# Attention outputs of six batches by seven products, with all slots of four engines in a written order

## The chip, the cores and the metric

The kernel runs on one NeuronCore of a Trainium2 chip, as a single program with one launch. The metric is device time in microseconds (us) of that core. Before the change three runs took 1434.19, 1436.90 and 1437.84 us, so the median is 1436.9 us. The profile is of one further execution, which took 1433.48 us with a span of 1431.7 us from its first to its last instruction.

A core has a matrix engine (PE, with PEld for its weight loads), a vector engine (DVE), a scalar engine (ACT), a general engine (POOL) and a queue that issues transfers (SP). Each works through its own instruction queue. Products are written to PSUM; in this program DVE and ACT take them out of it, and POOL works on SBUF alone.

## The reference, cut to what matters

Tokens are 8 batches of 512, each of 512 features, all float32. Two layers of cross attention stand in the network, each followed by a feed-forward part (a routed one after the first, a channel mix after the second). With a context of 120 keys for each batch and 16 heads of 32 features, a layer of attention is

```python
q = _split_heads(Q @ W_q.T)                  # Q is the layer norm of x
k = _split_heads(K @ W_k.T)                  # K and V are the context
v = _split_heads(V @ W_v.T)
scores = jnp.einsum('bhqd,bhkd->bhqk', q, k) / jnp.sqrt(jnp.float32(D_K))
probs = jax.nn.softmax(scores, axis=-1)
out = jnp.einsum('bhqk,bhkd->bhqd', probs, v)
out = out.transpose(0, 2, 1, 3).reshape(B, S, H * dk)
return out @ W_o.T                           # added to x, times tanh(gate)
```

The second layer adds biases and a mask over the keys. The change is about the last line, `out @ W_o.T`, and about the order in which everything in these two layers is issued.

## The kernel before, in words

**Tiling.** `x` stays in SBUF for the whole program as 32 tiles of 128 tokens, four to a batch. In a layer of attention (`CrossAttention`) keys and values are projected first (`project_keys`, `project_values`: one product of 120 x 512 for each batch), and then the tiles are worked through one by one.

**Queries.** For a whole batch they are computed by seven products of 256 x 256 blocks in place of eight (`SevenProducts`, Strassen's scheme in Winograd's form). `multiply` (line 149) issues four matmuls of 256 columns into one PSUM bank. The pieces `p1` to `p7` take the products out of PSUM and add them up. The sums of inputs that some products need (`left_steps`, `right_steps`) are made by DVE or POOL.

**Attention of a tile.** `scores` (line 489) fills two PSUM tiles of two banks each (pool `p_s`, two tiles in all, so one tile of tokens fills the pool). DVE takes the negative maxima (`nmx`, line 514) of the second of them, ACT runs eight exponentials over it (line 517), DVE takes the maxima (line 525) of the first and subtracts them (line 527), and ACT exponentiates the result (line 528). The step called `rest` takes reciprocals of the sums on DVE and multiplies on POOL (line 507, twice for a tile, 128 x 960 each). `transpose_probs` (line 546) turns the probabilities by 16 transposes into the same two PSUM tiles of `p_s`; `transpose_probs_late` (line 567) does so into four banks of the other pool, `p_mm`, which has four banks and serves everything else. `attend` (line 581) multiplies by the values, ACT copies the result to `aT` (line 589), and `output` (line 598) multiplies it with `wo`: four matmuls of 512 columns for each tile, after which DVE adds `gate` times the result to `x` (line 607).

**Slots.** `run` (line 617) is a loop of slots. Slot t holds the scores of tile t+1, a few products of queries of the next batch, the output of tile t-1 in two parts, the transposes and the attention of tile t, and the transposes of normalised `x` (`transpose_x`, line 421) of tile t+9. Between them `after(t, stage)` calls the next part of the network: in the first layer `RoutedFfn.in_slot` (statistics, the normalisation `route_norm` on ACT (line 714), transposes `route_x` (line 722) and logits `route_logits` (line 731), once for each tile); in the second `ChannelMix.in_slot`. `tail` works through the last slots.

**What sets the order.** `tc.manual_schedule(engines=...)` keeps the named engines in the order of the source. Around `run` it names PE alone in the first layer, and PE and SP in the second; a planner puts the instructions of DVE, ACT and POOL in order by its own estimate of when they can run. The construction before `run` and the tail behind it are in source order on the four compute engines.

Of the kernel before, what the change touches and what calls it, by code (L numbers as in the profile page):

```python
# [17 lines left out]
P = 128  # L18
# [53 lines left out]
class SevenProducts:  # L72
# [24 lines left out]
    @staticmethod  # L97
    def right_steps(w, t1, t2, t3, t4, engine):

        b11, b12, b21, b22 = [quarter(w, c, h) for c in (0, 1) for h in (0, 1)]

        def step(*args):
            return lambda: engine.tensor_tensor(*args)

        return [
            step(t3, b22, b12, ALU.subtract),  # L110
            step(t1, b12, b11, ALU.subtract),
            step(t2, b22, t1, ALU.subtract),
            step(t4, t2, b21, ALU.subtract),
        ]
# [91 lines left out]

class CrossAttention:
# [7 lines left out]
    def __init__(  # L215
# [20 lines left out]
        self.xn, self.xnT, self.qT, self.probs, self.aT = {}, {}, {}, {}, {}  # L236
        self.ops = {}
# [4 lines left out]
        with right("at_v") as self.vp:  # L242
            with right("at_k") as self.kp:
                self.load(ins, list(loads), mask, biases)
                if self.biased:
                    self.scale_biases()
                self.project_keys()
                if self.biased:
                    nc.gpsimd.tensor_scalar(self.gbo, self.gbo, self.gate, None, ALU.mult)
                for t in range(2):  # L250
                    self.normalize(t)
                if self.masked:
                    self.make_mask()
                self.sum_query_weights()
                for b in (1, 2):
                    self.stats_of_batch(b)
            self.work = pool("at_work", 2)
            self.prologue()

    def load(self, ins, loads, mask, biases):  # L260
# [4 lines left out]

        wv = self.soft.tile([P, NC * D], FP, name="wv", tag="pr")
        self.wv = wv.rearrange("p (c f) -> p c f", c=NC)
# [89 lines left out]
    def project_values(self, b):  # L357
# [15 lines left out]
        if b + 3 < B:  # L373
            self.stats_of_batch(b + 3)

    def prologue(self):

        for b in range(3):
            self.project_values(b)
        for t in range(2 * TB):  # L380
            self.transpose_x(t)
            self.normalize(t + 2)
            if t < TB - 1:
                self.project_values(t + 3)
            elif t < 2 * TB - 1:
                self.queries(0, t + 1 - TB)
        rest = self.scores(0)
        for b in range(B - 2, B):
            self.project_values(b)
        rest()  # L390

# [21 lines left out]
    def transpose_x(self, t):  # L413
        nc = self.nc
        b, i = divmod(t, TB)
        if i == 0:
            self.xnT[b] = self.work.tile([P, NC, S + 1], FP, name="xnT")
# [4 lines left out]
        nc.scalar.copy(self.xnT[b][:, :, i * P : (i + 1) * P], ps)  # L422
        if i == TB - 1:
            self.start_queries(b)
# [9 lines left out]

    def start_queries(self, b):

        xnT = self.xnT[b][:, :, :S]
        own = self.work.tile([P, 2, 256], FP, name="xns", bufs=1)
        sums = [quarter(xnT, 0, 1), quarter(xnT, 0, 0), own, quarter(xnT, 1, 0)]
        engine = self.nc.gpsimd if b > 1 else self.nc.vector  # L440
# [4 lines left out]
        self.xn7 = SevenProducts.right(xnT, *sums)  # L445

    def queries(self, b, f):

        if f == 0:
            self.qT[b] = self.work.tile([P, NC, S], FP, name="qT")  # L450
            self.q7 = SevenProducts(
                self.nc,
                lambda: self.p_mm.tile([P, 2, 256], FP, name="qps", tag="mm"),
                self.wq7,
                self.xn7,
                {(i, j): quarter(self.qT[b], i, j) for i in (0, 1) for j in (0, 1)},
                lambda: quarter(self.xnT[b], 0, 1),
                bias=(self.bqk[:, 0, 0:2], self.bmore) if self.biased else None,
            )
        self.q7.next(2 if f < TB - 1 else 1)  # L460
        if f == 0:
            for step in self.later_sums:
                step()

    def scores(self, t):
# [65 lines left out]
        def rest():  # L531
            norm(slice(2, 4))
            nc.vector.tensor_reduce(sm[:, :2, :], pv, AX.X, ALU.add)  # L533
            norm(slice(0, 2))
# [24 lines left out]
    def transpose_probs_late(self, t):  # L559
# [4 lines left out]
        for j in (2, 3, 0, 1):  # L564
# [3 lines left out]
            if j == 2:  # L568
# [5 lines left out]
    def attend(self, t):  # L574
# [13 lines left out]
        self.aT[t] = self.work.tile([P, NC, P], FP, name="aT")  # L588
        nc.scalar.copy(self.aT[t], aps)  # L589

    def output(self, t, chunks):

        nc, x = self.nc, self.cm.x
        if 0 in chunks:
            self.ops[t] = self.p_mm.tile([P, D], FP, name="ops", tag="mm")
        ops = self.ops[t]
        for c in chunks:
            nc.tensor.matmul(  # L598
                ops,
                self.aT[t][:, c, :],  # L600
                self.wo[:, c, :],
                start=(c == 0),
                stop=(c == NC - 1),
            )
        if NC - 1 in chunks:
            del self.ops[t], self.aT[t]
            nc.vector.scalar_tensor_tensor(
                x[:, t, :], ops, self.gate, x[:, t, :], ALU.mult, ALU.add
            )
# [7 lines left out]
    def run(self):  # L617

        for t in range(-1, NT - TB - 1):
            if t >= 0:  # L620
                if t + 10 < NT:
                    self.normalize(t + 10)
                self.scores(t + 1)()
            self.queries(*divmod(t + TB + 1, TB))
            self.after(t, 0)


            short = t % TB == TB - 2
            ahead = 3 if short else 2
            if t > 0:  # L630
                self.output(t - 1, range(ahead))
            x_ahead = short and not self.masked
            if x_ahead and t + 9 < NT:
                self.transpose_x(t + 9)
            if t >= 0:
                self.transpose_probs(t)
            if t > 0:
                self.output(t - 1, range(ahead, NC))
            if t + 9 < NT and not x_ahead:
                self.transpose_x(t + 9)  # L640
            self.after(t, 1)
            if t >= 0:
                self.attend(t)
            self.after(t, 2)

    def tail(self):

        for t in range(NT - TB - 1, NT + 1):
# [3 lines left out]
            self.output(t - 1, range(NC))  # L652
# [9 lines left out]
class RoutedFfn:  # L662
# [19 lines left out]

    def start(self):
# [22 lines left out]
    def route_stats(self, t):  # L706
        layernorm_sums(self.cm, self.route, t)
        layernorm_scales(self.cm, self.route, t, 1)

    def route_norm(self, t):  # L710

        nc, x = self.nc, self.cm.x[:, t, :]
        nc.sync.dma_start(out=self.aside[t * P : (t + 1) * P, :], in_=x)
# [41 lines left out]

    def in_slot(self, s, attention, stage):

        last = NT - TB - 1
        if stage == 2 and 0 <= s - 1:
            self.route_stats(s - 1)  # L760
        if (stage == 2 and (0 <= s - 1 < last - 1 or s == NT)) or (stage == 3 and s > last):
            self.route_norm(s - 1 if stage == 2 else s - 2)
        if stage != (0 if s == NT else 1):
            return
# [703 lines left out]
```

## Time and profile before

| what | us |
|---|---|
| median of three runs | 1436.9 |
| the profiled execution | 1433.48 |
| its span | 1431.7 |
| PE busy | 1384.2 (97%) |
| DVE busy | 1025.1 (72%) |
| ACT busy | 772.3 (54%) |
| POOL busy | 643.9 (45%) |
| one batch of the first layer's slots | 49.5 |
| one batch of the second layer's slots | 44.4 |

The first layer of attention lies from the start to about 475 us, the routed part up to 690 us, the second layer up to about 1138 us, and the channel mix behind that. The last two rows are the distance between the same instruction in two following batches (the products of queries that begin at 162.47, 212.01, 261.55 us in the first layer, and at 838.86, 883.22, 927.59 us in the second). A matmul's row in the profile is a little longer than its share of the time, since matmuls overlap; the distance between the starts of two rows is what a piece of work costs.

### The profile page before, as it was taken

To read this page: it belongs to the slowest core of one execution; us is meant where nothing else is said; L and a number is where in the kernel's file an instruction comes from. 1 tells how busy PE (TensorE), PEld (TensorE's weight loads), DVE (VectorE), ACT (ScalarE), POOL (GpSimd) and SP (SyncE) were. 2 spreads that over 40 slices of the span, in tenths; PEclk is the share of its full clock that TensorE was granted. 3 is DMA by queue.
4 is the path that set the end of the run, shared out by engine and by line. 5 is a ranking of instruction groups with operands and counts; after the bars stand their busy time and mean duration, and the time that the engine had idled before them with its cause. 6 is when DMAs were issued, how large, how long until landed. Compare 5 with 4: busy or idle time off the path is not lost.

```text
span 1431.7 us, 32559 instructions
## 1 busy us (share of the span) xinstructions
PE 1384.2 (97%) x13728; PEld 1068.2 (75%) x13728; DVE 1025.1 (72%) x1457; ACT 772.3 (54%) x1874; POOL 643.9 (45%) x576
## 2 busy tenths in 40 slices
PE   7999999999999998999999999999998999999997
PEld 3577777777776787888557777777776788888886
DVE  2666777777777676777576777777778588887786
ACT  1256666666666445444225665666656555445543
POOL 1425545545443001555375665665646333343331
PEclk9999999999999999999999999999999999999999
DMA  9200000000001347433301000000000000000001
GB/s 300 107 9 24 24 23 23 24 23 16 24 31 46 127 135 231 120 105 87 117 0 60 2 1 2 1 2 2 2 30 2 1 30 30 31 30 30 30 16 45
DMA packets 44886, 69.46 MB, mean 49 GB/s; under 512 B 2891, under 2 KB 20811, under 8 KB 44739
## 3 DMA queue, kind: packets, MB, share of 16 engines
q1 hardware_dynamic: 44451, 67.37, 14.6%
q8 instruction: 108, 1.77, 0.5%
q14 instruction: 39, 0.32, 0.1%
q10 hardware_dynamic: 288, 0.00, 0.0%
HBM read 50.59 MB, written 16.78 MB: 47 GB/s over the span
## 4 chain that ended last, share of the span: by engine, by line
PE 72%; DVE 14%; ACT 6%; POOL 4%; issue 3%; DMA 1%; POOLq 0%; DVEq 0%; ACTq 0%
PE ops L598 15%; PE qps L149 13%; PE tps L546 6%; PE cps L149 5%; PE aps L581 5%; PE s L489 4%; PE kps L342 4%; PE rps L992 3%; PE vps L361 3%; PE rlps L731 2%; PE l1ps L907 2%; PE ops L1013 2%; PE xnps L421 2%; PE l2ps L959 2%; PE gps L880 2%
## 5 line engine op out<-in xcount | busy, mean ns | idle before, releaser
L507 POOL TENSOR_TENSOR pr<-pr,rs 128x960 f32<-128x960 f32 x128 | 228.8, 1790 | 251.9 <-DVE rs L506 233.5
L598 PE MATMUL ops<-wo,aT 128*128 128x512 f32 x512 | 239.6, 594 | 0.7 <-ACT aT L589 0.7
L517 ACT ACTIVATE pr<-s,nmx 128x120 f32<-128x120 f32 x512 | 177.4, 372 | 114.0 <-DVE nmx L514 107.8
L598 PEld LDWEIGHTS ops<-wo,aT 128*128 128x128 f32 x512 | 92.1, 190 | 71.9 <-issue 67.0
L1005 POOL TENSOR_TENSOR r<-r,b 128x1024 f32<-128x1024 f32 x31 | 73.5, 2377 | 142.6 <-ACT r L1004 142.6
L149 PE MATMUL qps<-xnT,wq 128*128 128x256 f32 x512 | 119.6, 381 | 0.0
L546 PEld LDWEIGHTS tps<-ident,pr 128*120 128x120 f32 x864 | 96.8, 138 | 29.5 <-issue 26.2
L525 DVE TENSOR_REDUCE mx<-s 128x8 f32<-128x960 f32 x64 | 74.0, 1156 | 56.9 <-PE s L489 56.9
L517 ACT ACTIVATION_READ_ACCUMULATOR pr<-s,nmx 128x1 f32 x512 | 111.3, 217 | 0.0
L546 PE MATMUL tps<-ident,pr 128*120 128x128 f32 x864 | 104.7, 273 | 2.5 <-ACT pr L517 1.4
L149 PEld LDWEIGHTS qps<-xnT,wq 128*128 128x128 f32 x512 | 95.7, 189 | 15.2 <-issue 1.0
L533 DVE TENSOR_REDUCE sm<-pr 128x8 f32<-128x960 f32 x64 | 73.6, 1150 | 22.1 <-ACT pr L528 22.0
L49 DVE BATCH_NORM_STATS2 bnst<-x 128x6 f32<-128x512 f32 x128 | 86.8, 678 | 1.3
L422 ACT COPY xnT<-xnps 128x512 f32<-128x512 f32 x64 | 38.1, 595 | 82.0 <-PE xnps L421 82.0
L514 DVE TENSOR_REDUCE nmx<-s 128x8 f32<-128x960 f32 x64 | 73.5, 1149 | 6.8 <-PE s L489 6.8
L581 PE MATMUL aps<-prT,v 120*32 120x128 f32 x2048 | 73.3, 278 | 4.5 <-ACT prT L571 2.6
L527 DVE TENSOR_TENSOR pr<-s,mx 128x960 f32<-128x960 f32 x64 | 73.6, 1150 | 0.9
L1258 POOL TENSOR_TENSOR x<-x,cv 128x512 f32<-128x512 f32 x28 | 41.4, 1479 | 70.8 <-DVE cv L1255 70.8
L556 ACT COPY prT<-tps 120x1024 f32<-120x1024 f32 x54 | 55.0, 1019 | 32.9 <-PE tps L546 32.9
L489 PE MATMUL s<-kT,qT 32*128 32x120 f32 x2048 | 71.4, 276 | 0.0
L489 PEld LDWEIGHTS s<-kT,qT 32*128 32x128 f32 x2048 | 66.1, 187 | 6.5 <-issue 6.3
L581 PEld LDWEIGHTS aps<-prT,v 120*32 120x32 f32 x2048 | 53.8, 110 | 18.8 <-issue 8.3
(189 smaller groups left out, 3101.1 us busy)
## 6 DMA issues: line engine op xcount, KB each, us to landing
w<-in_w_dram SPq DMA_DIRECT2D x32, 512.0 KB, 4.8
x<-in_x_dram SPq DMA_DIRECT2D x8, 1024.0 KB, 15.4
aside<-x SPq DMA_DIRECT2D x32, 256.0 KB, 2.0
x<-aside SPq DMA_DIRECT2D x8, 1024.0 KB, 9.8
out_dram<-x SPq DMA_DIRECT2D x14, 512.0 KB, 2.8
ctx<-in_ctx_dram SPq DMA_DIRECT2D x4, 960.0 KB, 11.8
wk<-in_wk_dram SPq DMA_DIRECT2D x3, 1024.0 KB, 11.1
wv<-in_wv_dram SPq DMA_DIRECT2D x3, 1024.0 KB, 5.5
```

The source lines that it names most:

```text
L49: cm.nc.vector.bn_stats(st, cm.x[:, t, :])
L149: self.nc.tensor.matmul(ps[:, m, :], self.a[a][:, k, m * P : (m + 1) * P], self.b[b][:, k, :], start=(k == 0), stop=(k == 1),)
L489: nc.tensor.matmul(s[j // 2][:, j % 2, hc * LK : (hc + 1) * LK], self.qT[b][r : r + 32, hc, toks], self.kT[r : r + 32, hc, keys], start=no ...
L507: nc.gpsimd.tensor_tensor(pr[:, js, :, :], pr[:, js, :, :], rs[:, js, :, :].to_broadcast([P, 2, NC, LK]), ALU.mult,)
L514: nc.vector.tensor_reduce(nmx, sv[1], AX.X, ALU.max, negate=True)
L517: nc.scalar.activation(pr[:, 2 + j, hc, :], sv[1][:, j, hc, :], AF.Exp, bias=nmx[:, j, hc, :], accum_out=sm[:, 2 + j, hc : hc + 1],)
L525: nc.vector.tensor_reduce(mx, sv[0], AX.X, ALU.max)
L527: nc.vector.tensor_tensor(pv, sv[0], mx.to_broadcast([P, 2, NC, LK]), ALU.subtract)
L533: nc.vector.tensor_reduce(sm[:, :2, :], pv, AX.X, ALU.add)
L546: nc.tensor.transpose(ps[:, jj, hc * P : (hc + 1) * P], pr[:, 2 * u + jj, hc, :], self.cm.ident,)
L581: nc.tensor.matmul(aps[32 * j : 32 * j + 32, hc, :], self.v[b // 2][:LK, b % 2, h * HD : (h + 1) * HD], prT[:, j, hc, :], start=True, stop ...
L598: nc.tensor.matmul(ops, self.aT[t][:, c, :], self.wo[:, c, :], start=(c == 0), stop=(c == NC - 1),)
```

## The change

It has four parts.

1. **Outputs by seven products.** The outputs of batches 0 to 5 in each layer are no longer computed tile by tile. `aT` now holds the four tiles of a batch, and a new class, `SevenAdded`, multiplies it with `wo` by seven products, each scaled by the gate and added to `x`. Batches 6 and 7 keep `output`. The sums of `wo` are made once for each layer by POOL, in the buffer that held `wv`; the sums of `aT` are made by POOL in each of the six batches.
2. **A written order.** `run` is a list of slots of two kinds, `slot` and `short_slot`, and the four compute engines all follow the source.
3. **First slots.** The projections of the values of batches 4 to 7 move from ahead of the first slot into slots 0, 1 and 2; all seven products of the queries of batch 0 come one after another ahead of the scores; and `xnT` (normalised `x`, transposed) has one buffer in place of two.
4. **The next part of the network.** In the first layer `route_norm` of a tile moves to stage 0 of the slot in which `route_x` transposes it; the pieces of the routed part come two slots later than before and catch up at the end. In the second, statistics and transposes are spread differently over the last slots.

```diff
+class SevenAdded(SevenProducts):
+    def add(self, c, ps):
+        self.nc.vector.scalar_tensor_tensor(c, ps, self.gate, c, ALU.mult, ALU.add)
+    def add_sum(self, *places):
+        for c in places:
+            self.nc.gpsimd.tensor_tensor(c, c, self.t, ALU.add)
+    def p1(self):
+        ps = self.multiply("A11", "B11")
+        self.nc.scalar.activation(self.t, ps, AF.Copy, scale=self.gate)
+        self.add_sum(self.c[0, 0])
+    def p2(self):
+        self.add(self.c[0, 0], self.multiply("A12", "B21"))
+    def p5(self):
+        ps = self.multiply("S1", "T1")
+        self.add(self.c[0, 1], ps)
+        self.add(self.c[1, 1], ps)
+    def p6(self):
+        self.add(self.t, self.multiply("S2", "T2"))
+        self.add_sum(self.c[0, 1])
+    def p7(self):
+        self.add(self.t, self.multiply("S3", "T3"))
+        self.add_sum(self.c[1, 0], self.c[1, 1])
+    def p3(self):
+        self.add(self.c[0, 1], self.multiply("S4", "B22"))
+    def p4(self):
+        self.add(self.c[1, 0], self.multiply("A22", "T4"))
...
     def run(self):
+        self.slot(0, [(self.queries, 2), (self.project_values, 4)], [(self.queries, 1)])
+        self.normalize(2 * TB)
+        values = [(self.project_values, b) for b in (5, 6)]
+        self.slot(1, [(self.queries, 1)] + values, [(self.queries, 1)])
+        self.normalize(2 * TB + 1)
+        self.short_slot(
+            2, [(self.queries, 1)], [(self.project_values, B - 1), (self.end_of_values,)]
+        )
+        for b in range(B - 2):
+            t = TB * b + TB - 1
+            tile = TB * (b + 2)
+            last = b == B - 3
+            self.start_outputs(b)
+            outputs, queries = self.o7.next, self.queries
+            self.short_slot(
+                t,
+                [(self.transpose_x, tile), (self.normalize, tile + 2),
+                 (self.transpose_x, tile + 1)],
+                [(outputs,), (self.normalize, tile + 3), (self.transpose_x, tile + 2)],
+                [(queries, 1)],
+            )
+            self.slot(
+                t + 1,
+                [(outputs,), (self.transpose_x, tile + 3), (outputs, 2)],
+                [(outputs,)],
+            )
...
+            self.slot(
+                t + 2,
+                [(outputs,), (self.start_queries, b + 2), (outputs,), (queries, 1)],
+                [(queries, 1)] + [(self.output, t + 1)] * last,
+            )
...
+            self.slot(
+                t + 3,
+                [(queries, 3)],
+                [(queries, 1)] + [(queries, 1), (self.output, t + 2)] * last,
+            )
+
+    def end_of_values(self):
+        self.values.close()
+        self.sum_output_weights()
+        self.after(-1, 1)
+
+    def slot(self, t, ahead, behind):
+        rest = self.scores(t + 1)
+        self.issue(ahead)
+        self.after(t, 0)
+        rest(0)
+        self.transpose_probs(t)
+        rest(1)
+        self.issue(behind)
+        self.after(t, 1)
+        self.attend(t)
+        self.after(t, 2)
+
+    def short_slot(self, t, ahead, behind, first=()):
+        self.issue(first)
+        self.transpose_probs_late(t, (2, 3, 0))
+        self.issue(ahead)
+        self.attend(t)
+        if t % TB == TB - 1:
+            for step in self.output_sums:
+                step()
+        rest = self.scores(t + 1)
+        self.issue(behind)
+        self.after(t, 0)
+        self.after(t, 1)
+        rest(0)
+        rest(1)
+        self.after(t, 2)
...
-            with tc.manual_schedule(engines={engines.PE}):
+            with tc.manual_schedule(engines=compute):
                 attention.run()
-            with tc.manual_schedule(engines=compute):
                 attention.tail()
...
-        with tc.manual_schedule(engines={engines.PE, engines.SP}):
+        with tc.manual_schedule(engines=compute):
             attention.run()
-        with tc.manual_schedule(engines=compute):
             attention.tail()
             mix.run()
```

The prologue, `sum_output_weights` and `in_slot` of the routed part, in the new form:

```diff
     def prologue(self):
+        for b in range(2):
             self.project_values(b)
+        for t in range(TB):
             self.transpose_x(t)
             self.normalize(t + 2)
+            if t == 1:
+                self.project_values(2)
+        self.start_queries(0)
+        self.queries(6)
+        self.project_values(3)
+        self.queries(1)
+        for t in range(TB, 2 * TB):
+            self.transpose_x(t)
+            if t + 2 < 2 * TB:
+                self.normalize(t + 2)
+            if t == TB + 1:
+                rest = self.scores(0)
+        self.start_queries(1)
         rest()
+        self.stats_of_batch(B - 1)
...
+    def sum_output_weights(self):
+        w = self.wo
+        sums = self.xp.tile([P, 4, 2, 256], FP, name="wos", tag="xa")
+        sums = [sums[:, i] for i in range(4)]
+        for step in SevenProducts.right_steps(w, *sums, self.nc.gpsimd, negated=True):
+            step()
...
+        if stage == (0 if s < last else 3):
+            for t in self.tiles_ended(s - 1):
+                self.route_norm(t)
```

## The prediction

> **What bounds the kernel now.** I read the windows first: columns are the stretch, its length, then busy time of PE, PEld, DVE, ACT and POOL.
>
> ```profile
> 64.00:113.00 49.00, 46.24 (x350) 34.96 (x348) 32.58 (x44) 25.68 (x74) 16.91 (x14) 1.00 0.03 7
> 261.50:311.10 49.60, 49.60 (x481) 38.18 (x477) 35.43 (x57) 33.30 (x96) 25.31 (x26) 1.00 0.06 23
> 749.00:794.50 45.50, 43.89 (x377) 33.05 (x377) 29.84 (x41) 24.06 (x72) 27.64 (x20) 1.00 0.13 48
> 927.60:972.00 44.40, 44.40 (x441) 32.74 (x442) 32.80 (x46) 27.43 (x87) 27.68 (x23) 1.00 0.01 2
> ```
>
> The second and fourth rows are one batch of slots in each layer: PE is busy all the time, so work taken off PE is time won, and any wait put into PE's queue is time lost, one for one. The first and third are first slots, where PE has small holes. Next, PE's timeline:
>
> ```profile
> 94.30 1.89 PE L149 MATMUL qps<-xnT,wq 128*128 128x256 f32 x8
> 96.74 1.06 PE L546 MATMUL tps<-ident,pr 128*120 128x128 f32 x8 [0.55 <-DVE pr L527]
> 98.47 1.09 PE L546 MATMUL tps<-ident,pr 128*120 128x128 f32 x8 [0.68 <-ACT pr L517]
> ...
> 285.16 1.99 PE L149 MATMUL qps<-xnT,wqs 128*128 128x256 f32 x8
> 287.00 1.89 PE L149 MATMUL qps<-xnT,wq 128*128 128x256 f32 x8
> 288.72 1.88 PE L598 MATMUL ops<-wo,aT 128*128 128x512 f32 x4
> 290.44 1.91 PE L546 MATMUL tps<-ident,pr 128*120 128x128 f32 x16
> ```
>
> Starts give costs: a product of seven 1.72 us (287.00 to 288.72; 1.83 behind scores), half an output of a tile 1.72. The upper rows show what PE can't outrun: 3.7 us of work behind the scores was too little for the two score tiles to be drained. How long draining takes is in DVE's, ACT's and POOL's timelines:
>
> ```profile
> 286.34 1.15 DVE L514 TENSOR_REDUCE nmx<-s 128x8 f32<-128x960 f32 x1
> 287.40 1.15 DVE L527 TENSOR_TENSOR pr<-s,mx 128x960 f32<-128x960 f32 x1
> ```
> ```profile
> 287.52 0.36 ACT L517 ACTIVATE pr<-s,nmx 128x120 f32<-128x120 f32 x1 [1.64 <-DVE nmx L514]
> 290.24 1.04 ACT L528 ACTIVATE pr<-pr 128x960 f32<-128x960 f32 x1
> 291.13 0.62 ACT L179 COPY xnT<-qps 128x512 f32<-128x512 f32 x1
> ```
> ```profile
> 33.56 1.27 POOL L88 TENSOR_TENSOR wqs<-wq 128x512 f32<-128x512 f32 x1
> 34.91 1.27 POOL L88 TENSOR_TENSOR wq<-wq 128x512 f32<-128x512 f32 x1
> 293.85 1.79 POOL L507 TENSOR_TENSOR pr<-pr,rs 128x960 f32<-128x960 f32 x1 [1.28 <-DVE rs L506]
> ```
>
> Maxima 1.15, eight exponentials 2.72 (287.52 to 290.24), the long one 0.89, a sum on POOL 1.35 from start to start, a multiplication of probabilities 1.79. With `nmx` first, as the source has it, the score tiles are free 3.95 us after the scores end (0.08 + 1.15 + 2.72; the other one earlier: two reductions and the subtraction, 3.4).
>
> **The change, part by part. (1) Seven products.** A batch loses 4 x 3.43 = 13.72 us of PE and gains 7 x 1.72 = 12.04: −1.68, for 12 batches **−20.2 us**. Off PE, a batch adds three DVE operations (seven where four were, 0.74 each), one ACT copy, and eight POOL operations: four sums of `aT` and four additions into `x`, 1.2 to 1.5 each (rows of 128 x 512 on POOL run from 1.09 to 1.48), near 10.5 us. POOL then has 38 of 44 us in a batch of the second layer. That fits, so it costs only where PE waits for POOL.
>
> **(2) The short slot, first layer.** Its queues in written order: PE has scores(t+1), product 1, `transpose_x`, logits, `route_x`, scores(t+2). `route_x` reads what `route_norm` writes in the same slot, and on ACT that stands behind eight exponentials, the long one, product 1's copy, a normalisation and a copy. From the end of the scores: 0.08 + 1.15 + 2.72 + 0.89 + 0.55 + 0.72 + 0.49 + 0.82 = 7.4 us. PE has 1.83 + 0.44 + 0.89 = 3.2 us to fill it. PE waits 4.2, in five batches (the first one has nothing to route yet): **+21.0**. In the other slots the same pair is 10 us apart and hidden. What is queued behind is PE's whole queue; nothing else becomes late, DVE and POOL catch up.
>
> **(3) The short slot elsewhere** (first batch of layer 1, six of layer 2). Only product 1 and `transpose_x`, 2.27 us, stand between two scores; the score tiles are free after 3.95. PE waits 1.7, seven times: **+11.9**. So the short slot gives back what seven products won.
>
> **(4) POOL in the second layer.** In the slot behind, `transpose_probs` wants both multiplications of the tile. Count from the end of scores(t+1). On ACT product 1's copy ends at 5.35 (0.08 + 1.15 + 2.72 + 0.89 + 0.5); POOL, done with its four sums by then, adds it to `x` (1.3), then a bias (line 410, 1.3), then does two multiplications (3.6): 11.55. PE passes scores(t+2) at 5.1, then products 2, 5, 6 and a `transpose_x` (1.83 + 1.72 + 1.72 + 0.44): 10.8. The wait is 0.75; none with additions of 1.1 on POOL, 1.5 with 1.5. I take 0.8, six times: **+4.8**. In layer 1 the wait of (2) covers it.
>
> **(5) First slots, in each layer.** (a) Queries in a run: product 6 needs sums that stand on DVE behind a value copy and four tiles of statistics (3.2 us); PE waits 1.7 (1.1 before). (b) scores(1) follow scores(0) with two `transpose_x` between (0.9), and DVE has a value's statistics and an addition ahead of `nmx` (1 us): 4.0. (c) Behind scores(1) DVE has two sums of queries (1.4) that wait for ACT's last `xnT` copy (0.85 in), a reduction (1.07), `nmx` and `mx` (1.07 each), two of the last batch's statistics woven between (0.8 each) and the subtraction (1.15): it ends at 8.25, where PE has two products and a projection, 6.9: a wait of 1.3. The copy of the turned probabilities stands behind more of the same and ends at 13.9, PE is there at 11.8: 2.1. (d) `sum_output_weights`: POOL's four sums write over `wv`, so they wait for the last projection of values (end V), and the multiplications of tile 3 are queued behind them. PE has one product (1.7) and then wants them. By the nearest rows, sums of `wq` on POOL, 4 x 1.35 = 5.4, then 2 x 1.8: the transposes end at V + 9.9 with the last two groups of 0.9 us, in place of V + 3.5: 6.4. The Trainium skill ("GPSIMD Engine Reference", section 3.1) gives such an addition 4497 ns for 2048 elements, so an estimate of 1.12 for 512: 4.5 us and a wait of 5.5. Rows with the other layout (line 107, 1.10) side with it. I take 6.0 between. Sum 1.7 + 4.0 + 1.3 + 2.1 + 6.0 = 15.1, two layers 30.2. What goes are the holes that were there: 1.1 + 0.55 + 0.7 + 0.4 + 0.9 = 3.6 in layer 1 and 2.6 in layer 2. Net **+24.0**.
>
> **(6) A rule that speaks against the change.** The Trainium skill ("SBUF — State Buffer", section "SBUF: two separate sides") says that a DVE operation with two SBUF inputs and a POOL operation that reads SBUF lock each other out for the whole instruction. The trace shows it:
>
> ```profile
> 89.32 1.49 DVE L107 TENSOR_TENSOR xnT<-xnT 128x512 f32<-128x512 f32 x1
> 294.11 0.75 DVE L607 SCALAR_TENSOR_TENSOR x<-ops,gates,x 128x512 f32<-128x512 f32 x1 [0.40 <-PE ops L598]
> ```
>
> The first ran beside a multiplication on POOL (88.47 to 90.26) and took 1.49 instead of its usual 0.69; the second, with one input in PSUM, started inside the one shown above at 293.85 and took 0.75. The new DVE operations are of the second kind. Read broadly, as a lock between any two such operations, the rule would cost up to 84 x 0.8 = 67 us if all stood on PE's path; by the row, nothing. I take nothing.
>
> **(7) The rest** (loads, routed part, mix, tail): same instructions; outputs of tiles 24 and 25 move into PE's queue in slots with enough cover. Bounds −1 and +4, nothing taken.
>
> Sum: −20.2 + 21.0 + 11.9 + 4.8 + 24.0 = +41.5. The profiled execution took 1433.5 (span 1431.7 and 1.8 around it), so 1475 for such an execution; the median of the three runs is 3.4 above it. I say **1476**.
>
> **Rivals.** *A. Score tiles cost no wait (the other side).* Place: the second scores of a short slot and of the first slots. If their release, and what ACT has behind it, kept up with PE, 32.9 us of (2) and (3) and 2 x (4.0 + 1.3) of (5) fall away: 41.5 − 43.5 = −2, and with POOL's waits at their low end −8: 1425 to 1432. It decides from where draining falls from 3.95 to 2.3 us. For it: the holes of before are under 1 us. Against it: those stood behind 3.7 us of PE work, not 2.3. 7%.
> *B. The first slots are lighter than laid out*: DVE's order there has the most pieces, and my positions add up errors. With a third of (5) left: 1460. 20%.
> *C. POOL becomes the bound*: at 1.5 for every added operation and locks of 0.7 beside DVE's, its 38 us pass 45 in layer 2, and its backlog reaches the transposes in all slots: about 2 us more in each of 11 batches: 1498. 17%.
> *D. Gains and waits cancel* (A in part): within 0.3%. 2%.
> My forecast, 1465 to 1488, has the rest, 54%.
>
> **How the numbers follow.** 0.3%, about 4 us, is what a measurement of this kernel can tell from no change. Slower holds my forecast, B and C: 91%. A gives faster, 7%; D the 2%. The range: C's upper part (above 1495) and A and D with the lowest part of B are left out, some 2 in 10: 1453 to 1495.
>
> **What would show it.** The windows of a batch: about 52 us in layer 1 (49.5 before) and 44.5 to 45.5 in layer 2 (44.4). PE rows: `rxps` with a wait of about 4 us for ACT's normalisation once a batch; `s` with about 1.7 for the exponentials; the fourth tile's `tps` with 4 or more for POOL in the first slots. DVE's operations on line 218 near 0.7. If PE is busy without a hole in the short slots, (2) and (3) are wrong and the time is near 1430; if batches of layer 2 pass 47 us, it is C.

## The result and the profile after

Four runs of the changed kernel took 1500.48 to 1505.53 us, median 1504.65; runs of the kernel before on the same chip had a median of 1436.18. The ratio is 1.0465 (95% interval 1.0446 to 1.0483): 68 us slower. The forecast was 1476, with a range of 1453 to 1495. The direction was right; the forecast was 29 us too low, and the result lies outside its range.

The profiled execution took 1505.5 us, with a span of 1503.7. First the windows of the changed kernel that answer to the four shown of before. The columns are again the stretch, its length and the busy time of PE, PEld, DVE, ACT and POOL; of the last three, the first is the granted clock of PE.

```profile
75.00:133.20 58.20, 49.82 (x426) 36.24 (x424) 37.87 (x58) 26.83 (x88) 25.22 (x22) 0.88 0.02 6
233.97:288.95 54.98, 50.68 (x505) 44.67 (x501) 39.46 (x62) 33.02 (x97) 35.22 (x34) 0.94 0.06 21
801.60:860.50 58.90, 50.41 (x446) 36.49 (x445) 38.74 (x60) 27.10 (x89) 30.43 (x27) 0.88 0.10 37
952.60:998.12 45.52, 43.55 (x468) 37.08 (x464) 35.53 (x51) 27.50 (x89) 37.54 (x31) 1.00 0.01 2
```

Rows one and three are first slots (scores of tile 0 or 1 up to those of tile 4), row two is a batch of the first layer, row four one of the second. A batch takes 55.0 us in the first layer (49.5 before, forecast 52) and 45.5 to 46.5 in the second (44.4 before, forecast 44.5 to 45.5; the row shown is one of 45.5). In the stretches where the forecast fell short the clock column reads 0.88 to 0.94, where it read 1.00 before. Next, the list of PE's waits (what it waited for, us in total, times, the longest):

```profile
PE rxps L865 <- ACT x L857: 21.4, 5, 4.3
PE tps L633 <- POOL pr L571: 10.7, 2, 5.4
PE s L543 <- DVE pr L591: 9.8, 7, 2.5
...
PE s L553 <- DVE pr L591: 3.9, 2, 2.6
...
PE qps L149 <- POOL ve L58: 1.9, 1, 1.9
PE tps L612 <- POOL pr L571: 1.9, 4, 0.5
PE qps L149 <- POOL rstd L59: 1.9, 1, 1.9
PE s L543 <- ACT pr L581: 1.8, 7, 0.3
```

These are the waits of the forecast, each at its place: `route_x` for `route_norm` (21.4; forecast 21.0), tile 3's transposes for the sums on POOL (10.7; 12.0), the scores for their PSUM tiles (15.5 in all, of which 5.1 stand at scores(1) of the two layers), the first queries (1.9 each; 1.7). None is longer than forecast by more than 0.4 us in all. Most of what the forecast lacks is in the rows behind them. PE's timeline of one short slot of the first layer (start, us, the instructions, and in brackets the wait ahead of them):

```profile
242.66 1.11 PE L865 MATMUL rxps<-ident,x 128*128 128x128 f32 x4 [4.27 <-ACT x L857]
243.56 1.06 PE L941 MATMUL pps<-ident,permT 128*128 128x128 f32 x4
244.55 2.08 PE L553 MATMUL s<-kT,qT 32*128 32x120 f32 x32
246.56 2.43 PE L149 MATMUL qps<-wo,aT 128*128 128x256 f32 x8
...
258.63 1.17 PE L553 MATMUL s<-kT,qT 32*128 32x120 f32 x32
```

Behind the wait the 32 matmuls of the scores take 2.08 us; a slot later, without a wait ahead, the same 32 take 1.17. Two groups of four transposes take 0.9 to 1.0 from start to start where 0.53 is usual. The same shows in the first slots:

```profile
80.50 2.60 PE L553 MATMUL s<-kT,qT 32*128 32x120 f32 x32 [2.59 <-DVE pr L591]
83.02 5.70 PE L149 MATMUL qps<-xnT,wq 128*128 128x256 f32 x16
...
127.56 3.71 PE L633 MATMUL tps<-ident,pr 128*120 128x128 f32 x16 [5.34 <-POOL pr L571]
```

Two products took 5.70 us here (3.62 in the prologue), the 16 transposes 3.71 (1.91 in the slots behind). PE runs there at half its rate. The windows around the wait of 4.27 us (238.39 to 242.66) show when; again the first figure after POOL is the granted clock:

```profile
237.24:240.65 3.41, 1.15 (x11) 0.95 (x9) 2.78 (x7) 3.41 (x15) 2.78 (x3) 1.00 0.00 0
240.65:244.06 3.41, 1.41 (x7) 1.41 (x8) 1.61 (x4) 2.15 (x5) 3.27 (x3) 0.50 0.00 0
244.06:247.48 3.42, 3.42 (x37) 2.79 (x36) 0.76 (x1) 0.97 (x2) 2.56 (x4) 0.50 0.00 0
247.48:250.89 3.41, 3.41 (x19) 2.98 (x19) 3.28 (x4) 2.97 (x17) 0.00 (x0) 1.00 0.00 0
```

### The profile page after: what moved, and what is told of

Read it like the earlier page. It is cut to its first block, busy times and chain, and to the rows that moved or that the text cites. A ratio compares the mean times of both kernels' runs of the same rounds, so it can differ in the third digit from the quotient of the medians.

```text
span 1503.7 us, 33436 instructions
## 1 busy us (share of the span) xinstructions
PE 1401.9 (93%) x14016; PEld 1144.8 (76%) x14016; DVE 1063.1 (71%) x1521; ACT 768.8 (51%) x1886; POOL 772.8 (51%) x680
## 4 chain that ended last, share of the span: by engine, by line
PE 65%; DVE 14%; ACT 9%; POOL 6%; issue 4%; DMA 1%; POOLq 0%; ACTq 0%; DVEq 0%
PE qps L149 20%; PE tps L612 5%; PE cps L149 5%; PE aps L647 4%; PE s L553 4%; PE ops L665 3%; PE kps L390 3%; PE rps L1152 3%; ACT pr L581 3%; PE vps L409 3%; PE tps L633 3%; PE l1ps L1067 2%; PE ops L1173 2%; PE gps L1040 2%; DVE rT L1132 2%
## 5 line engine op out<-in xcount | busy, mean ns | idle before, releaser
L149 PE MATMUL qps<-xnT,wq 128*128 128x256 f32 x512 | 125.0, 389 | 0.0
L222 POOL TENSOR_TENSOR x<-x,qT 128x512 f32<-128x512 f32 x48 | 60.8, 1278 | 77.1 <-DVE qT L218 64.7
L553 PE MATMUL s<-kT,qT 32*128 32x120 f32 x2048 | 81.0, 296 | 4.0 <-DVE pr L591 3.9
L553 PEld LDWEIGHTS s<-kT,qT 32*128 32x128 f32 x2048 | 73.3, 204 | 11.0 <-issue 10.5
L612 PEld LDWEIGHTS tps<-ident,pr 128*120 128x120 f32 x640 | 71.7, 137 | 9.2 <-POOL pr L571 3.5
L612 PE MATMUL tps<-ident,pr 128*120 128x128 f32 x640 | 76.6, 273 | 1.9 <-POOL pr L571 1.9
L58 POOL TENSOR_SCALAR ve<-mv 128x1 f32<-128x1 f32 (+1 forms) x56 | 14.5, 259 | 114.1 <-DVE mv L50 111.1
L622 ACT COPY prT<-tps 120x1024 f32<-120x1024 f32 x40 | 40.5, 1013 | 59.6 <-PE tps L612 59.6
L592 ACT ACTIVATE pr<-pr 128x960 f32<-128x960 f32 x64 | 66.4, 1038 | 1.2 <-DVE pr L591 1.2
## 6 DMA issues: line engine op xcount, KB each, us to landing
x<-aside SPq DMA_DIRECT2D x8, 1024.0 KB, 10.5
```

The lines of the kernel that those rows point to most:

```text
L149: self.nc.tensor.matmul(ps[:, m, :], self.a[a][:, k, m * P : (m + 1) * P], self.b[b][:, k, :], start=(k == 0), stop=(k == 1),)
L553: nc.tensor.matmul(s[j // 2][:, j % 2, hc * LK : (hc + 1) * LK], self.qT[b][r : r + 32, hc, toks], self.kT[r : r + 32, hc, keys], start=no ...
L612: nc.tensor.transpose(ps[:, jj, hc * P : (hc + 1) * P], pr[:, 2 * u + jj, hc, :], self.cm.ident,)
```

## The experiments

The theory after the result: the waits stand as forecast, and each long one also takes the granted clock down for a while, which is the missing part of the sum. The rivals: PE's rows are slow because the other engines catch up there; POOL is the bound (rival C of the forecast); PE has more work than counted. Each kernel ran beside the one before on its chip; the medians of before there lie between 1434.9 and 1437.8, so a difference of some 3 us between two experiments says little.

### Filling the waits with useless work

In the five short slots of the first layer that wait for `route_norm`, PE gets 3.4 us of products that nobody reads (`fill` is 8 there, and 0 in every other slot):

```diff
     def route_x(self, t, ps, at=None, fill=0):
+        for _ in range(fill):
+            nc.tensor.matmul(
+                ps[:, :256], at.wo[:, 0, :P], at.wo[:, 0, :256], start=True, stop=True)
         for c in range(NC):
```

> Does the granted clock cost time behind a wait? In the short slot of the first layer (five batches) eight useless products of 128x128 by 128x256 (2 x 1.72 = 3.4 us of PE work) go ahead of route_x, where PE waited 4.3 us for ACT's route_norm. They give nothing to wait for and the wait ends when it did. Theory (PE at rest loses clock, and 3.4 us run at half rate afterwards): the wait on rxps falls to about 0.9, pps, scores and products behind it go back to full rate, and 2.3 us a batch are won: 11.5 in all, 1493. Rival 1 (PE rows behind the wait are slow because DVE, ACT and POOL catch up there and hold something that PE needs): the rows stay slow, 1504. Rival 2 (POOL's backlog bounds the batches): 1504 too, and the time comes back as a longer wait on tps.

Measured: 1492.54 (1486.74 to 1495.35), 12.1 us less than the changed kernel, with more work in it. PE's timeline of that kernel, in the same short slot:

```profile
235.61 3.62 PE L864 MATMUL rxps<-wo 128*128 128x256 f32 x16
240.04 0.66 PE L869 MATMUL rxps<-ident,x 128*128 128x128 f32 x4 [0.81 <-ACT x L857]
240.54 0.60 PE L946 MATMUL pps<-ident,permT 128*128 128x128 f32 x4
241.07 1.17 PE L553 MATMUL s<-kT,qT 32*128 32x120 f32 x32
```

The useless products end 0.8 us ahead of ACT's result, so the wait ends when it did; the scores behind it are back at 1.17. DVE, ACT and POOL have the same to catch up as before, so the rival that blames them is out. A second kernel keeps this and fills the other waits too, in `slot`, `short_slot` and `prologue`; `fill(n)` issues n useless products of 128 x 128 by 128 x 256 into a bank of its own:

```diff
     def slot(self, t, ahead, behind):
+        n = 5 if t == 0 else 3 if t % TB == 0 and (self.masked or t == TB) else 0
+        if n:
+            self.fill(n)
         rest = self.scores(t + 1)
...
         self.issue(first)
+        if t == TB - 1:
+            self.fill(12)
         self.transpose_probs_late(t, (2, 3, 0))
...
-        self.queries(6)
+        self.queries(2)
+        self.fill(4)
+        self.queries(4)
         self.project_values(3)
```

> The changed kernel in its own order, with useless products of 128x128 by 128x256 (0.43 us each) in every wait of PE that the change brought: eight ahead of route_x (five batches of the first layer), three ahead of the second scores of the other short slots (wait 1.3 to 1.5), five ahead of scores(1) (2.6), four between the second and third product of the first queries (1.9), twelve ahead of the turning of tile 3 (5.4). No wait ends sooner, so every microsecond that is won is time at half rate behind a wait. The windows of the changed kernel count 37.4 us of lost clock (1 less the granted clock, times the length), 4.1 before the change; 6.7 of the 37.4 lie in the experts, which are not touched here and where it may fall otherwise. Theory: 27 us are won, 1478 (1473 to 1484). Rival 1 (the clock costs only what the fill in the five short slots won, 12 us): 1491 to 1494. Rival 2 (the missing part of the sum is PE's own added work): 1500 to 1505.

Measured: 1485.94 (1481.88 to 1487.92), so 18.7 less by the medians; the two profiled executions differ by 23.6 in span. That is past rival 1 and rival 2, and short of the 27 expected. Where the rest went shows when PE's timelines are added up from row to row (start of a row to the start of the next, less the wait stated with it):

| profiled execution | rows | waits | without the fill |
|---|---|---|---|
| before | 1385.7 | 26.9 | |
| changed | 1403.4 | 80.2 | |
| all waits filled | 1420.2 | 39.9 | 1375.2 (17.7 ahead of `route_x`, 27.3 elsewhere) |

The rows of the changed kernel fell from 1403.4 to 1375.2 at full rate: 28.2 us, as expected. But the waits are only 40.3 us less, where 45.0 us of fill went in: 4.7 came back. One place is plain in PE's timeline of the filled kernel:

```profile
92.29 1.08 PE L649 MATMUL aps<-prT,v 120*32 120x128 f32 x32 [1.82 <-DVE prT L622]
```

This is the second wait of the forecast's (c), put there at 2.1 us. In the changed kernel it is absent, since PE, slowed behind scores(1), arrived late enough not to wait.

How long must a wait be? In the traces of before, of the changed kernel and of the nine experiments, take every wait of PE that has no other of 0.4 us or more within 10 us of it, and the lost clock (1 less the granted clock, times the length) of the window from its start to 9 us past its end:

| length of the wait, us | waits | of these with lost clock | mean loss, us |
|---|---|---|---|
| near 0.5 | 89 | 0 | 0 |
| near 1.0 | 49 | 12 | 0.4 |
| near 1.5 | 5 | 0 | 0 |
| near 2.0 | 31 | 14 | 0.8 |
| near 2.5 | 12 | 11 | 2.2 |
| 4.3 | 15 | 15 | 2.8 |
| 5.4 | 8 | 8 | 3.4 |

The loss is always 0, about 1.7 or about 3.4 us: one or two stretches of 3.4 us at half rate. Many of these waits are the same place in several kernels, so the counts are not independent trials. All 12 losses near 1.0 are at second scores of the second layer, where a wait of 1.2 us has another of 0.25 close behind it.

What decides it can be read from the clock record. In each trace the half-rate stretches start at whole multiples of 3.41 us from each other, so the clock is set window by window. Count PE's rest (time without a matmul's row) in each window that ran at full rate, from 25 us on, in all eleven traces. Below 1.2 us of rest, none of 4355 windows was followed by one at half rate; from 1.2 to 2.0, 36 of 122; from 2.0 us on, all 60. So a wait of 2 us that falls across the edge of two windows costs nothing, and a wait of 4 us or more always puts 2 us into one of them. The four windows shown above fit: the first has 2.26 us of rest, the second 2.00, the third none.

### route_norm ahead of the scores

```diff
     def short_slot(self, t, ahead, behind, first=()):
+        self.after(t, 0)
         rest = self.scores(t + 1)
         self.issue(behind)
-        self.after(t, 0)
         self.after(t, 1)
```

> route_norm of the short slots is issued ahead of the scores, so that on ACT it stands ahead of the exponentials. Theory (waits plus the clock they cost): the 21.4 us of waits on rxps go, and 5 x 2.3 us at half rate with them; POOL's multiplications are then late for transpose_probs in five batches, as forecast for layer 2 (0.8 each, +4): 1504.6 - 21.4 - 11.5 + 4 = 1476 (1472 to 1480). Waits alone, with the clock lower for another reason: 1487. Rival (POOL is the bound): a wait on tps for POOL of 3 or more takes the place of the wait on rxps: 1495 to 1502.

Measured: 1474.90 (1474.57 to 1476.79), 29.8 less, as the theory had it. The wait on `rxps` for ACT is gone from PE's list; the new one is four times 0.85, and it is not the expected one for POOL:

```profile
PE pps L941 <- DVE rs L570: 3.4, 4, 0.9
```

A batch of the first layer takes 49.3 us in place of 55.0, with a granted clock of 1.00. Of 30 us won, the waits explain 18 (21.4 less 3.4). The rest, 12, is what filling the same five waits had won, so it is put down to the clock.

### The sums of the output weights, later

Two kernels issue `sum_output_weights` behind the short slot of tile 2, the first on DVE, the second on POOL:

```diff
         self.short_slot(2, ..., [..., (self.end_of_values,)])
+        self.sum_output_weights()
     def end_of_values(self):
         self.values.close()
-        self.sum_output_weights()
```

> sum_output_weights is issued after the short slot of tile 2, behind the multiplications of tile 3 in time, and on DVE in place of POOL (4 x 0.7 us). Theory: the wait of 5.4 us on tps for POOL goes in each layer, and with it 1.8 us at half rate: 2 x 7.2 = 14.4, so 1490. Waits alone: 2 x 5.4 = 10.8, so 1494. Rival (POOL is full anyhow, the next tile's probabilities are late by as much): 1501 to 1505.

Measured: 1501.78 (1500.74 to 1502.81), 2.9 less where 14 were expected. PE's timeline and DVE's of this kernel:

```profile
120.67 1.09 PE L633 MATMUL tps<-ident,pr 128*120 128x128 f32 x8 [1.12 <-POOL pr L571]
122.95 0.65 PE L633 MATMUL tps<-ident,pr 128*120 128x128 f32 x4 [1.19 <-POOL pr L571]
125.55 1.11 PE L633 MATMUL tps<-ident,pr 128*120 128x128 f32 x4 [1.95 <-DVE qT L203]
```

```profile
120.61 2.84 DVE L107 TENSOR_TENSOR wos<-wo 128x512 f32<-128x512 f32 x2
123.48 1.42 DVE L107 TENSOR_TENSOR wos<-wo,wos 128x512 f32<-128x512 f32 x2
124.81 0.68 DVE L203 TENSOR_TENSOR qT<-qT,qps 128x512 f32<-128x512 f32 x1
```

The sums were now ahead of the operation that frees a bank of `p_mm`, and PE waited for that. And the two multiplications alone make PE wait 1.1 and 1.2, which the expectation had left out. On POOL, which rested 7.5 us there, it should be better:

> sum_output_weights behind the short slot of tile 2, now on POOL, where the run with the sums on DVE showed 7.5 us of rest behind tile 3's multiplications. Theory: of the two waits of 5.4 on tps, 1.1 + 1.2 for the multiplications themselves stay; 3.1 go in each layer, and some 0.9 at half rate: 8 in all, 1496.5. On DVE the sums stood ahead of two operations that free banks, which cost 2.0 of the gain and a wait at half rate: here they don't. Rival (the next tile's multiplications or product 5 are then late behind the sums): 1501 to 1505.

Measured: 1497.37 (1492.61 to 1498.24), 7.3 less, as expected. So of the wait of 5.4 the sums made some 3; the remainder is there without them, since PE has too little work between the scores and the transposes of tile 3.

### Two products between the scores

```diff
-            "1256374",
+            "2156374",
...
-                [(outputs,), (self.normalize, tile + 3), (self.transpose_x, tile + 2)],
+                [(outputs, 2), (self.normalize, tile + 3), (self.transpose_x, tile + 2)],
...
-                [(outputs,), (self.transpose_x, tile + 3), (outputs, 2)],
+                [(self.transpose_x, tile + 3), (outputs, 2)],
```

> Products 2 and 1 (in this order) both stand in the short slot; transpose_x of the fourth tile leads the slot behind. So 4.0 us of PE work stand between the two scores, where 2.3 stood. Theory: the waits of scores for the exponentials go where they stood in a batch (some 10.5 us of the 15.5 listed, the rest stands at scores(1) of each layer), with some 3 us at half rate behind them, and the wait on rxps is 1.7 shorter in five batches (8.6), still with half rate behind it: 1504.6 - 22 = 1482; if the shorter wait of 2.5 no longer lowers the clock, 1471. Rival (POOL's backlog): product 1 reaches POOL later, transpose_probs waits for it instead: 1495 to 1505.

Measured: 1489.89 (1481.83 to 1492.32), 14.8 less where 22 were expected. PE's waits in this kernel:

```profile
PE rxps L865 <- ACT x L857: 12.7, 5, 2.5
PE tps L633 <- POOL pr L571: 10.7, 2, 5.4
...
PE tps L612 <- POOL pr L571: 7.6, 6, 1.3
PE xnps L473 <- ACT xn L461: 7.3, 9, 1.0
```

The waits of scores in the batches are gone and the one on `rxps` is 1.7 shorter, as expected. Of what they won, 12 us came back: the turned `x` of the fourth tile, now first in the slot, waits for ACT (7.3 in place of 0.8), and `transpose_probs` waits for POOL (7.6 in place of 1.9), as the rival said, though not for as much.

### The written order without the seven products

Each slot has the whole output of the tile before (slots 1 and 2 those of tiles 0 and 1); `start_outputs`, `SevenAdded` and the sums of the output weights go:

```diff
-            outputs, queries = self.o7.next, self.queries
+            outputs, queries = self.output, self.queries
...
-                [(outputs,), (self.normalize, tile + 3), (self.transpose_x, tile + 2)],
+                [(outputs, t - 1), (self.normalize, tile + 3), (self.transpose_x, tile + 2)],
...
-                [(outputs,), (self.transpose_x, tile + 3), (outputs, 2)],
-                [(outputs,)],
+                [(outputs, t), (self.transpose_x, tile + 3)],
+                [],
...
-                [(outputs,), (self.start_queries, b + 2), (outputs,), (queries, 1)],
+                [(outputs, t + 1), (self.start_queries, b + 2), (queries, 1)],
...
-                [(queries, 3)],
+                [(outputs, t + 2), (queries, 3)],
```

> The written order is kept, the seven products are undone: each slot has the whole output of the tile before (3.4 us of PE, no sums on POOL, no sums of the output weights). Theory (the waits come from the little work between two scores and from POOL's sums): PE work +1.5 us a batch (+17.6); the waits of second scores go (-10.4, and -1.7 at half rate); the wait on rxps is 1.7 shorter in five batches (-8.6, and -3 at half rate); tile 3's tps waits 3.1 less in each layer, with 1.8 at half rate (-10); POOL's waits of layer 2 go (-1.9): 1504.6 - 18 = 1487. Rival (the waits belong to the order alone and stay, the seven products won 20): 1520 to 1525.

Measured: 1490.42 (1487.73 to 1493.63), 14.2 less than with the seven products. In this order the part of the change that takes work off PE makes the kernel slower. With whole outputs PE's waits are 62.7 us in place of 80.2: 10.0 for 21.4 on `rxps`, since the work that the seven products take away covered the short slot, and 3.8 for 10.7 on tile 3's `tps` for POOL, which has no sums to make.

This kernel is also 53.4 us slower than the one before on its chip. So the written order, with its first slots and its places for the routed part but without seven products for the outputs, already costs most of what the change costs. Seven products in the order of before were not run.

### All mended

The parts above that helped, together: `route_norm` first, products 2 and 1 between the scores, the sums on POOL behind tile 3, and a projection of values moved between scores(0) and scores(1). Product 1's addition on POOL is put off until product 5, and the fourth tile's `transpose_x` stands between products 5 and 6. Beyond the edits shown already:

```diff
+        self.project_values(4)
         self.start_queries(1)
         rest()
...
-        self.slot(0, [(self.queries, 2), (self.project_values, 4)], [(self.queries, 1)])
+        self.slot(0, [(self.queries, 2), (self.project_values, 5)], [(self.queries, 1)])
...
-        values = [(self.project_values, b) for b in (5, 6)]
+        values = [(self.project_values, b) for b in (6,)]
...
         self.nc.scalar.activation(self.t, ps, AF.Copy, scale=self.gate)
-        self.add_sum(self.c[0, 0])
...
         self.add(self.c[1, 1], ps)
+        self.add_sum(self.c[0, 0])
```

> The changed kernel with its waits mended: route_norm ahead of the scores in the short slot; products 2 and 1 both between its two scores, and product 1's addition on POOL put off until product 5; sum_output_weights on POOL behind tile 3's multiplications; the projections of values one slot earlier, so that one stands between scores(0) and scores(1). Theory (each wait plus the clock behind it): from 1504.6 go 29.7 (the run with route_norm first), 3.4 (waits on pps left there), 10.4 and 1.7 (second scores and their windows at half rate), 2 x 4 (tps of tile 3) and 2 x 5 (scores(1)): 1441, between 1435 and 1447; mean granted clock above 0.99. Rival (the waits only move, POOL or DVE being the bound): 1455 to 1470. If seven products win their 20 us in full and no wait is left: below 1425.

Measured: 1460.23 (1457.72 to 1462.70), 1.0160 times before (1.0143 to 1.0177). The clock is as expected (0.995), the time is 19 over: the rival's case. POOL's timeline of a short slot of the second layer, and PE's behind it:

```profile
912.34 1.27 POOL L466 TENSOR_TENSOR x<-x,gbo 128x512 f32<-128x512 f32 x1 [1.17 <-ACT xn L462]
913.58 3.53 POOL L572 TENSOR_TENSOR pr<-pr,rs 128x960 f32<-128x960 f32 x2
...
919.11 1.26 POOL L222 TENSOR_TENSOR x<-x,qT 128x512 f32<-128x512 f32 x1
```

```profile
917.16 1.96 PE L613 MATMUL tps<-ident,pr 128*120 128x128 f32 x16 [1.67 <-POOL pr L572]
918.96 1.89 PE L149 MATMUL qps<-wo,qT 128*128 128x256 f32 x8
922.41 1.08 PE L648 MATMUL aps<-prT,v 120*32 120x128 f32 x32 [1.56 <-DVE prT L621]
```

POOL isn't full; it stands with the addition of a bias (line 466) that must wait for ACT's `normalize`, and the multiplications that PE wants are queued behind. The addition that was put off came at 919.11, behind statistics too; DVE's addition of product 6 waits for it, and the copy of the turned probabilities stands behind that. So both new waits come from the places of two POOL instructions. The last kernel moves them (`settle` is product 1's addition on POOL), and puts the statistics of batch 5 behind four products of the first queries:

```diff
-                 (self.transpose_x, tile + 1)],
-                [(outputs, 2), (self.normalize, tile + 3), (self.transpose_x, tile + 2)],
+                 (self.transpose_x, tile + 1), (self.normalize, tile + 3)],
+                [(outputs, 2), (self.transpose_x, tile + 2)],
...
         rest(1)
+        if t % TB == TB - 1:
+            self.o7.settle()
         self.after(t, 2)
...
-        self.queries(6)
+        self.queries(4)
+        self.stats_of_batch(5)
+        self.queries(2)
         self.project_values(3)
```

> The mended kernel, with three more edits for the waits that its trace shows: normalize of the fourth tile is issued ahead of the scores of the short slot (POOL's bias addition stood there waiting for ACT, with tile 4's multiplications behind it), product 1's addition on POOL follows directly behind those multiplications and ahead of the statistics (DVE's addition of product 6 waited for it, with the copy of the turned probabilities behind), and the statistics of batch 5 are put behind four products of the first queries. Theory (the waits of 1.67 and 1.56 in six batches of layer 2 and its first, 0.5 in five batches of layer 1, 1.9 and 1.8 at half rate in a first slot go): 1460.2 less 22 to 28: 1432 to 1438, so about even with the kernel before. Rival (POOL's and DVE's queues leave no room and the waits move again): 1450 to 1460.

Measured: 1446.69 (1443.72 to 1450.44), 1.0083 times before (1.0063 to 1.0103): 13.5 less than the kernel ahead of it, of 22 to 28 expected. The two waits shrank, and another is there:

```profile
PE tps L617 <- DVE pr L596: 8.8, 11, 1.2
PE tps L638 <- POOL pr L576: 5.0, 4, 2.3
PE aps L652 <- DVE prT L625: 3.5, 2, 1.8
```

The turned probabilities go into the score tiles, and with POOL in time these are what is late: DVE's subtraction has not let go of them, eleven times 0.8 us. In the second layer the batch is back at 44.5 us, what it took before (44.4). In this kernel PE's rows add up to 1377.6 us and its waits to 47.6: 8.1 less work than before, and 20.7 more waits. None of these kernels beats the one before.

## Why the prediction was right and wrong

Against before, the span of the changed kernel has 72.0 us more. By the table of rows and waits these are 53.3 of waits, 28.2 of rows at half rate, and 10.5 less of PE's own work at full rate (1385.7 to 1375.2): 71.0. The forecast had 61.7 of waits, nothing for the clock, and 20.2 less of work. Its waits were 8.4 too many and its saving 9.7 too large; that these two nearly cancel is luck, and what is left of the miss is the clock.

**The step that failed** is the one that priced waits, in (2), (3) and (5): "PE waits 4.2, in five batches: +21.0" and its like. A wait was counted by its own length, at the full rate behind it. The forecast even read the granted clock, 1.00 in all its windows, and took it as given. By the table of waits above, one of 4.3 loses another 2.8, so five of them 14 (filling them won 12.1); the two of 5.4 another 6.8; those at scores(1) another 4. The Trainium skill ("TensorE: Matmul & The Clock Gate", "Part 1: The HAM clock gate") says that PE runs at half its clock after an idle window of about 3.4 us, and gets it back after about as long a busy one. The traces agree on the half and on the steps of 1.7 us lost, which is half of 3.4. They do not agree that it takes 3.4 us of rest: eleven of twelve waits of 2.5 us cost a step, and 14 of 31 waits of 2.0; 2.0 us of rest in one window of 3.41 was enough in 60 of 60. By the page alone, an estimate for the nine waits that the forecast itself put at 4.0 or more (`route_x` five times, scores(1) and tile 3 twice each) is at most 9 x 1.7 = 15 us, and the forecast 1491: half of what was missing.

**(1) Seven products** won less than 20.2. In the last kernel the 196 products in all take 350.5 us from start to start; the 112 of before take 199.7. So the 84 added ones cost 150.8, or 1.80 each, not 1.72; the 48 whole outputs that they replace cost 164.9 (220.9 less 56.0), or 3.44 each. That is 14.1. A product that follows scores or an attention costs 1.83, and the new order has more of these. The scores and the transposes of `x` cost 2.9 more in this order.

**(2)** was right to the tenth in the wait, 21.4, and lacked about 12 us of clock. Its chain is in ACT's timeline of the changed kernel, with the exponentials first and `route_norm` last, where the forecast had it:

```profile
236.39 0.36 ACT L581 ACTIVATE pr<-s,nmx 128x120 f32<-128x120 f32 x1 [1.60 <-DVE nmx L578]
...
239.10 1.04 ACT L592 ACTIVATE pr<-pr 128x960 f32<-128x960 f32 x1
239.99 0.72 ACT L226 ACTIVATE qT<-qps,gates 128x512 f32<-128x512 f32 x1
240.56 0.85 ACT L461 ACTIVATE xn<-x,nmr,rstd 128x512 f32<-128x512 f32 x1
241.27 0.62 ACT L474 COPY xnT<-xnps 128x512 f32<-128x512 f32 x1
241.73 0.87 ACT L857 ACTIVATE x<-x,nmr,rstd 128x512 f32<-128x512 f32 x1
```

**(3)** forecast 11.9; the waits of second scores that aren't scores(1) come to 10.4 (15.5 less 5.1). The forecast took the exponentials for what ends the wait. They end only its last part: PE first wants the tile that DVE's subtraction drains.

```profile
910.71 0.38 PE L543 MATMUL s<-mbias,ones 1*128 1x480 bf16 x2 [1.21 <-DVE pr L591]
911.33 0.38 PE L543 MATMUL s<-mbias,ones 1*128 1x480 bf16 x2 [0.25 <-ACT pr L581]
```

**(4)** forecast 4.8; it was 1.9. **(5)** (a) 1.9 for 1.7; (b) 2.6 and some 0.4 on the transposes between, for 4.0; (c) did not occur while PE was slow, and half of it did when it wasn't; (d) 5.4 for 6.0, with four sums in 5.1 us on POOL, between the two prices that were weighed. But (d) put all of the wait to the sums, and the run with them moved shows that some 2 us are there without.

**(6)** was right to take nothing for the ports. Of DVE's 84 new additions in the changed kernel, 60 have the row below (shortest, median, longest, in ns), and the other 24 took 740 to 751. They keep their length, though POOL is busy in 35 of the 55 us of a batch:

```profile
L218 DVE SCALAR_TENSOR_TENSOR x<-qps,gates,x x60: 707/744/752, 144.2 to 1114.6; 128x512 f32<-128x512 f32 x60
```

**(7)** took nothing for the experts, whose instructions are the same. In the changed kernel two windows at half rate there cost 3.4 us (not the 6.7 that the expectation of the last fill put there), and PE waits once for 2.1 us (`rxps` for ACT) where it did not before; before, no window there was at half rate. With the other waits filled this part took 308.9 us from the last scores to the next layer's first, in place of 314.4.

Of the rivals, A is out: the score tiles did cost their wait. B is out as a time, though (c) was overestimated. C's time, 1498, is near the measured one, but not its mechanism: batches of the second layer stay at 45.5 to 46.5, and POOL still rests.

## What to carry to other kernels

When PE has been busy without a hole, price a new wait at its length and what the clock takes behind it: by these runs nothing at 0.5 us, about 1 us at 2, 2 at 2.5 and about 3 from 4 on; the granted clock, and one and the same row behind a wait and away from it, show it. Taking work off the bounding engine wins only where the other engines are ahead by as much; where the work covers a wait, put other work in its place first.

## What was not expected of the hardware

Useless matmuls in a wait made the program faster, by 12 us in five places and by 19 in all, with 45 us of products that nobody reads. And 1.3 us of rest in one window of 3.41 us could be enough for a stretch at half rate, while 1.9 us in another cost nothing.
